# Two fused image layers on one core: the last image's output projection in strips of eight neighbouring rows, with the third image's fusion beside the last convolutions

## The chip, the cores and the metric

The kernel runs on one core of a Trainium2 chip. The metric is the device time of one execution in microseconds; "before" is the median of three runs. A profile is taken of one further execution. Engines: TensorE (PE: matrix products), VectorE (DVE), ScalarE (ACT), GpSimd (POOL) and SyncE (SP, which here only issues DMA transfers). Each engine works through its own instructions in order; POOL issues DMA transfers too.

## What is computed

All arrays are float32; x is (4, 512, 64, 64): four images. Layer 0 is a linear-attention block, layer 1 an edge-map block on its result. Cut to what matters:

```python
# layer 0 (64 heads of 8 channels)
qkv = 1x1 projections of x                                  # 1536 channels
pw  = grouped_1x1(depthwise_5x5(qkv))                       # the convolution branch, 64 more heads
f   = concat(qkv, pw) as (heads, 24, N)                     # 128 heads
query, key, value = relu(f[:8]), relu(f[8:16]), f[16:]
scores = [value; 1] @ key.T                                 # sums over all N = 4096 positions
out = (scores @ query)[:8] / (scores @ query)[8]            # per head and position
y   = batchnorm(proj_1x1(out, 1024 -> 512)) + x
# layer 1
sobel, lap, diag, grad = four 3x3 edge maps of each channel of y (square roots, absolutes, a maximum)
ef  = concat(gelu(bn(w_branch[k] @ map[k])) for the four maps)   # 4 x 128 channels
att = sigmoid(w_att2 @ gelu(w_att1 @ mean(ef over the image)))   # needs the whole image
z   = w_fuse @ (ef * att) + b_fuse
out = gelu(channel_layernorm(z)) + y
```

Two sums over a whole image order the work: `scores` must be complete before any position can be projected, and the mean of `ef` must be complete before the fusion `z` can begin.

## The kernel before

**Passes.** Sixteen passes, a `Group(b, g)` for each of four images and four groups of 16 heads. A pass runs over eight strips of 512 positions and does the 1x1 projections (`project`), the value products, the transposes (`turn`) and the scores. Its convolution branch runs one pass later: `rest()` lists 21 numbered steps (convolutions of KEY and QUERY by halves of the image, transposes `ctr`, correlations `corr`, denominators, `conv_divide`, folding with the projection weights) that are placed between the following pass's steps. After the last pass nothing follows, so the last group's 21 steps form a tail of their own (`tail`).

**Finished images.** For each image `stages()` makes three generators: `project_out` (the 1024 to 512 projection, with batch norm and residual; 8 strips of 4 output chunks), `edge_branches` (edge maps and the four branch products) and `fuse_out` (attention weights, fusion, layer norm, output). For the first three images they are advanced in small steps "behind" the next image's passes: each step of a pass costs a nominal time, `advance(t * pace)` adds it to an account, and background steps run while the account is positive. Their nominal shares are `SHARE_Y` 90, `SHARE_E` 450, `SHARE_F` 100 and some waits, 736 an image. One `pace` serves all passes from the second image on; it is set such that the third image's edges end within the tail and its fusion is left over.

**Last image.** After the tail the last image's stages run with `side="left"` in other tile pools, interleaved by hand: the first 16 of the 32 projection chunks alone, then the other 16 and the third image's fusion (`fill`, with the `FILL_` constants) between 16 edge steps, then the rest.

**Orders.** The order of instructions on PE is the order in which the program issues them. SP, POOL, DVE and ACT are ordered by a scheduler with priorities. `dve` and `act` are wrappers for operations put forward (all of them show as line 121), `nc.vector` and `nc.gpsimd` are plain.

**Strips.** x, and with it q, k, v, is held in strips of every fourth row: strip (half, k) is the rows k, k+4, ... of one half of the image, eight rows of 64. `project_out` goes by such strips: `load(j)` fetches `hd` (plain queries, from `flat_q`, one transfer of 1 MB) and four `chd` (convolved heads, from `cheads`, 256 KB each) and the residual `xr`; `attend(hd, 0)` is ReLU on ACT (L683), denominators `den` on PE (L686) and a reciprocal on DVE; `attend(hd, 1)` spreads the reciprocals by a product (`over`, L693) and multiplies `hd`. Then, for each chunk, eight products `yps` (L723), a scalar-tensor-tensor to `yt` and a store to `y` through POOL's queue (L734). `conv_divide` (around L576) is what writes `cheads`. The edges load windows `win` of neighbouring rows of `y` (L756), so with strips of every fourth row they need four strips of a half to be out first.

**Edges and fusion.** An edge step has eleven DVE instructions (L778 to L805), four on ACT (L792 to L806) and branch products `br` (L812, two groups of 3.43 us for one step of the last image); a GELU gives `ef_o`, stored to `ef` through POOL's queue (L825). The attention weights start with `hid_ps` (L897). The fusion has four product groups `zps` a strip (L929), a square `sq` on ACT, a copy `z`, running sums `total`, the product `var` (L945), a reciprocal `rstd` (L948), a scaling (L956), GELU (L957), the residual add with `yr` (L960) and the store (L961). For the third image (`b == B - 2`) the sums run on POOL and the copy `z` on ACT.

Of the kernel before, what the change touches and what calls it, by code (L numbers as in the profile page):

```python
# [70 lines left out]
FILL_Y, FILL_F = 6.9, 2.95  # L71
FILL_FIRST, FILL_ATT = 34.0, 18.0
FILL_EACH = (16 * FILL_Y + 40 * FILL_F - FILL_FIRST - FILL_ATT) / (4 * NJ // 2 - 1)

LEFT_E = 14.0
# [16 lines left out]
def conv_seq_kernel(  # L92
# [162 lines left out]
    class Group:  # L255
# [315 lines left out]
        def conv_divide(self, half):  # L571
            banks = self.spread_out(self.crec)
            for i in range(4):
                q = work_tile("cq")
                dve.tensor_mul(q, self.conv[QUERY][i], banks[i])
                nc.sync.dma_start(out=self.cheads[half, self.g, i], in_=q)  # L576
# [3 lines left out]
        def rest(self):  # L580

            h0, h1 = self.halves

# [12 lines left out]
            def roll(t, half):  # L596
# [10 lines left out]
                8: [cv(KEY, h1), roll(QUERY, h0)],  # L607
# [4 lines left out]
                13: [cv(QUERY, h0), roll(QUERY, h1)],  # L612
                14: co(h1, 1, 0),
                15: [*co(h1, 1, 2), own("conv_denominators", h0), own("mix")],
                16: [own("conv_weights")],
                17: [own("conv_divide", h0), own("conv_heads")],
                18: [cv(QUERY, h1), own("conv_fold")],
                19: [own("conv_denominators", h1)],
                21: [own("conv_divide", h1)],
# [28 lines left out]
    def project_out(b, ks, cheads, folded, side):  # L648
# [4 lines left out]
        with ExitStack() as stack:  # L653
            pool = stack.enter_context(tc.tile_pool(name=f"Y{b}", bufs=1, side=side, reuse_waits="tile"))
# [7 lines left out]
            def load(j):  # L662
                half, k = STRIPS[j]
                r, at = (k + 2) % 4, 8 * half + (k + 2) // 4
                q = pool.tile([P, NG, 512], F32, name="hd", tag="hd", bufs=3 if side == "right" else 2)
# [4 lines left out]
                for g in range(NG):  # L670
                    t = pool.tile([P, 512], F32, name="chd", tag="chd", bufs=6 if side == "right" else 4)
# [6 lines left out]
            def attend(hd, part):  # L678

                if part == 0:  # L680
# [6 lines left out]
                    recs[:] = [pool.tile([P, 512], F32, name="hrec", tag="hrec")]  # L687
# [3 lines left out]
                for g in range(NG):  # L691
                    q = slice(32 * g, 32 * g + 32)
                    nc.tensor.matmul(banks[g], lhsT=spread[q, :], rhs=recs[0][q, :], start=True, stop=True)  # L693
                for g in range(NG):
                    dve.tensor_mul(hd[g], hd[g], banks[g])

            recs = []
# [7 lines left out]
            ahead = load(1) if side == "right" else None  # L705
# [5 lines left out]
            for j, (half, k) in enumerate(STRIPS):  # L711
                hd = following
                following, ahead = ahead or (load(j + 1) if j + 1 < NJ else None), None
                if side == "right" and j + 2 < NJ:
                    ahead = load(j + 2)
                for c in range(NCH):
# [18 lines left out]
                    yield SHARE_Y / (NJ * NCH)  # L735

    def edge_branches(b, efs, pool_sb, side):

        y = ys[b % 2]
        with ExitStack() as stack:  # L740
# [24 lines left out]
            def edges(u, pair):  # L765
# [41 lines left out]
                if u + 1 < steps:  # L807
# [9 lines left out]
            def store(u, ks, parts):  # L817
# [7 lines left out]
                nc.gpsimd.dma_start(out=efs[wide * u // 512][:, ks[0] : ks[1] + 1 : step, at : at + wide], in_=o)  # L825
# [9 lines left out]
            if side == "left":  # L835

                load(0, 0)
                load(0, 1)
                banks = None
                for n in range(2 * steps + 1):  # L840
                    made = edges(n // 2, n % 2) if n < 2 * steps else None
# [31 lines left out]
    def fuse_out(b, efs, pool_sb, side):  # L873

        y = ys[b % 2]
        with ExitStack() as stack:
# [49 lines left out]
            def fuse(c, ef, zs, total, n):  # L926
# [6 lines left out]
                if b == B - 2:  # L933
# [4 lines left out]
                if c:  # L938
                    (dve if b == B - 1 else gps).tensor_add(total, total, sq)

            def norm(piece, zs, total):
# [8 lines left out]
                for c in range(NCH):  # L950
# [9 lines left out]
                    nc.gpsimd.tensor_add(rows(z), rows(z), rows(yr, WB)[:, :, 1 : W + 1])  # L960
# [5 lines left out]
            for piece in pieces + [None]:  # L966
                if piece:
# [9 lines left out]
                    fuse(0, ef, zs, total, n)  # L977
                    yield share
                    fuse(1, ef, zs, total, n)
# [3 lines left out]
                if piece and late:  # L983
                    fuse(2, ef, zs, total, n)
# [4 lines left out]
                if piece:  # L989
                    for c in range(3 if late else 2, NCH):  # L990
                        fuse(c, ef, zs, total, n)
# [3 lines left out]
    def stages(last, side="right"):  # L995
# [6 lines left out]
            project_out(b, ks, last.cheads, last.folded, side), edge_branches(b, efs, pool_sb, side),  # L1002
# [5 lines left out]
    for b in range(B):  # L1008
        cheads = dram.tile([2, NG, 4, P, 512], F32, name="cheads")
# [17 lines left out]
    def run(steps):  # L1027
# [9 lines left out]
    tail = [  # L1037
        (1, (4.0, 0.0)), (2, (2.0, 2.0, 2.0)), (3, (2.0, 2.0)), (4, (1.0, 1.0, 1.0)), (5, (1.0, 1.0)), (6, (1.0, 1.0)),
        (7, (1.0, 1.0)), (8, (4.0, 0.0)), (9, (2.0, 2.0, 2.0)), (10, (2.0, 2.0, 0.0)), (11, (1.0, 1.0)), (12, (1.0, 1.0)),
        (13, (4.0, 0.0)), (14, (1.0, 1.0)), (15, (1.0, 1.0, 2.0, 2.0)), (16, (3.0,)), (17, (3.0, 3.0)), (18, (6.0, 3.0)),  # L1040
        (19, (10.0,)), (21, (4.0,)),
    ]
    each = SHARE_Y + SHARE_E + SHARE_F + WAIT_Y + 2 * WAIT_E + WAIT_F + 6.0
    start = sum(t for t, _ in passes[NG]) - 3 * T_PROJ
    pace = ((B - 1) * each - SHARE_F - WAIT_F - 6.0 - LEFT_E) / (
        sum(t for steps in passes[NG:] for t, _ in steps) - start + sum(sum(v) for _, v in tail)
    )
# [10 lines left out]
    for n, steps in enumerate(passes):  # L1058
# [3 lines left out]
        run(steps)  # L1062
# [4 lines left out]
    for n, much in tail:  # L1067
        for (_, step), t in zip(others[n], much, strict=True):
            step()
            advance(t * pace)  # L1070
# [3 lines left out]
    projected, edged, fused = stages(last, "left")  # L1074
    next(edged)
    for _ in range(3):
        next(projected)
    while len(behind) > 1:
        if next(behind[0], None) is None:
            behind.pop(0)  # L1080
    next(behind[0])
    for n in range(NCH * NJ // 2):
        next(projected)
        if n in (4, 8, 12):
            next(behind[0])
    rest, spent, given = [projected] + behind, 0.0, 0.0

    def fill(much):

        nonlocal spent, given  # L1090
        given += much
        while rest and spent < given:
# [114 lines left out]
```

## Time and profile before

| | us |
|---|---|
| median of three runs (4747.78 to 4751.59) | 4748.3 |
| the profiled execution | 4767.75 |
| its span | 4765.8 |
| PE busy / DVE / ACT / POOL | 4523.5 / 2105.1 / 1619.2 / 1061.4 |
| mean granted TensorE clock | 0.975 |

The span runs from the first to the last instruction of the profiled execution. A profile's windows give each engine's busy time in a stretch, and the clock that TensorE was granted; its waits say which engine stood for whose result, and for how long in total; its groups give, for a line and an operation, the count, the busy time, the mean duration of one and the idle time just before them with what ended it. Where each stage begins is read off the timeline of PE: the first instruction of the last convolutions at 3887.46 us, the first `yps` of the last image at 4065.70, its last at 4346.2, the first `hid_ps` of the last image at 4598.97. PE's instructions come in records; a group of four 512-wide products is eight of them.

### The profile page before, as it was taken

What the parts mean: (1) busy time and instruction counts of PE and PEld (TensorE: products, weight loads), DVE (VectorE), ACT (ScalarE), POOL (GpSimd) and SP (SyncE); (2) the same over time, 40 slices, a digit from 0 to 9 for tenths busy, and PEclk for the clock granted to TensorE, in tenths of its full rate; (3) what the DMA queues carried; (4) which work ended last, traced back from release to release, by engine and by line L of the source; (5) the groups of instructions that cost most, each with busy time, mean ns of one, the idle gap of its engine ahead of it and who ended that gap; (6) DMA issues with size and microseconds to landing.
All of it is one profiled execution on the core that took longest, in us unless ns stands there. A gap on an engine that the chain in (4) does not pass through costs nothing. (4 is left out here: it accounts for less than half of the span.)

```text
span 4765.8 us, 85177 instructions
## 1 busy us (share of the span) xinstructions
PE 4523.5 (95%) x35900; PEld 2485.1 (52%) x35900; DVE 2105.1 (44%) x2788; ACT 1619.2 (34%) x2737; POOL 1061.4 (22%) x1387
## 2 busy tenths in 40 slices
PE   9999999999999999899999999999999996999787
PEld 5565554445666654444566665544455653443333
DVE  1212212225566535222466644323246565378666
ACT  1111111003554424200345553410034543136575
POOL 2121211111121125211111213511111121113543
PEclk9999999999999999999999999999999997999898
DMA  8677796656777776865687877786477776554345
GB/s 235 170 188 192 208 257 169 170 131 186 195 213 204 217 202 209 236 155 147 173 214 204 218 211 213 211 220 184 126 188 197 191 196 168 149 156 135 124 129 174
DMA packets 433388, 889.63 MB, mean 187 GB/s; under 512 B 181192, under 2 KB 213992, under 8 KB 414576
## 3 DMA queue, kind: packets, MB, share of 16 engines
q1 hardware_dynamic: 343024, 588.17, 45.9%
q0 software_dynamic: 89984, 296.03, 22.5%
q8 instruction: 283, 4.64, 0.4%
q14 instruction: 97, 0.79, 0.1%
HBM read 635.17 MB, written 248.84 MB: 185 GB/s over the span
## 5 line engine op out<-in xcount | busy, mean ns | idle before, releaser
L299 PE MATMUL proj<-xt,w_sb 128*128 128x512 f32 x2048 | 943.4, 604 | 8.8 <-DMA xt<-in_x 5.6
L299 PEld LDWEIGHTS proj<-xt,w_sb 128*128 128x128 f32 x2048 | 374.9, 191 | 451.1 <-issue 427.5
L418 PE MATMUL cv<-rolled,mat 64*32 64x504 f32 (+2 forms) x10240 | 559.0, 584 | 7.9 <-DMA rolled<-flatq 6.1
L327 PEld LDWEIGHTS val<-w_sb,xt 128*128 128x128 f32 x4096 | 480.5, 195 | 51.9 <-issue 35.7
L812 PE MATMUL br<-maps,wbr_sb 128*128 128x256 f32 (+1 forms) x1792 | 483.4, 424 | 22.6 <-ACT maps L806 10.2
L121 ACT COPY strip<-proj 128x512 f32<-128x512 f32 x256 | 149.5, 584 | 1037.0 <-PE proj L299 988.5
L929 PE MATMUL zps<-ef,wf_sb 128*128 128x512 f32 (+1 forms) x1056 | 461.7, 590 | 37.9 <-ACT z L121 22.8
L327 PE MATMUL val<-w_sb,xt 128*128 128x128 f32 x4096 | 494.2, 280 | 2.4 <-DVE kc_sb L121 1.8
L723 PE MATMUL yps<-chd,fold_sb 128*128 128x512 f32 x1024 | 465.9, 598 | 3.1 <-DVE s_sb L121 2.3
L723 PE MATMUL yps<-hd,fold_sb 128*128 128x512 f32 x1024 | 460.3, 592 | 0.0
L812 PEld LDWEIGHTS br<-maps,wbr_sb 128*128 128x128 f32 x1792 | 346.1, 196 | 168.1 <-issue 95.7
L121 DVE SCALAR_TENSOR_TENSOR yt<-yps,shift,xr 128x512 f32<-128x512 f32 x128 | 96.0, 751 | 725.3 <-PE yps L723 698.1
L418 PEld LDWEIGHTS cv<-rolled,mat 64*32 64x32 f32 x10240 | 197.7, 107 | 332.8 <-issue 326.5
L473 PE MATMUL corr<-near,ckt 128*32 128x160 f32 x8192 | 340.4, 315 | 15.4 <-ACT co L121 8.2
L929 PEld LDWEIGHTS zps<-ef,wf_sb 128*128 128x128 f32 x1056 | 200.8, 193 | 281.4 <-issue 226.9
L734 POOL DMA_DIRECT2D y<-yt x128 | 114.6, 895 | 960.0 <-DVE yt L121 839.1
L723 PEld LDWEIGHTS yps<-hd,fold_sb 128*128 128x128 f32 x1024 | 194.6, 190 | 244.9 <-issue 244.4
L723 PEld LDWEIGHTS yps<-chd,fold_sb 128*128 128x128 f32 x1024 | 188.9, 190 | 246.0 <-issue 227.6
L473 PEld LDWEIGHTS corr<-near,ckt 128*32 128x32 f32 x8192 | 265.4, 111 | 89.8 <-issue 54.1
L121 ACT ACTIVATE kt<-tr 128x512 f32<-128x512 f32 x128 | 75.9, 593 | 626.5 <-PE tr L351 468.8
L121 DVE COPY vt<-val 128x512 f32<-128x512 f32 x128 | 87.4, 683 | 392.0 <-PE val L327 382.4
L121 ACT ACTIVATE co<-cv 128x256 f32<-128x256 f32 (+1 forms) x384 | 162.3, 455 | 278.9 <-PE cv L418 256.1
(135 smaller groups left out, 5121.0 us busy)
## 6 DMA issues: line engine op xcount, KB each, us to landing
near<-near SPq DMA_DIRECT2D x256, 528.0 KB
xt<-in_x SPq DMA_DIRECT2D x172, 512.0 KB
rolled<-flatk POOLq DMA_DIRECT2D x256, 256.0 KB, 7.2
rolled<-flatq POOLq DMA_DIRECT2D x256, 256.0 KB, 7.4
win<-y SPq DMA_DIRECT2D x96, 396.0 KB
near<-vt SPq DMA_DIRECT2D x512, 66.0 KB
y<-yt POOLq DMA_DIRECT2D x128, 264.0 KB, 6.3
flatk<-strip POOLq DMA_DIRECT2D x128, 256.0 KB, 5.7
```

The source lines that it names most:

```text
L121: self.last = getattr(self.engine, name)(*args, **kwargs)
L299: nc.tensor.matmul(ps, lhsT=self.w[t][:, c, :], rhs=xs[self.b, j][c], start=(c == 0), stop=(c == NCH - 1))
L327: nc.tensor.matmul(ps[:, ts(c, P)], lhsT=xs[self.b, j][n][:, ts(c, P)], rhs=self.w[VALUE][:, n, :], start=(n == 0), stop=(n == NCH - 1),)
L418: nc.tensor.matmul(rows(banks[2 * s + i])[32 * j : 32 * j + 32, :, c0:c1], lhsT=self.mat[t][q, 4 * s + j, (dx + 2) * 4 : (dx + 2) * 4 + 4, :],
L473: nc.tensor.matmul(self.banks[jj][32 * i : 32 * i + 32, 160 * b : 160 * b + 160], lhsT=self.held["c", i][:, at : at + 32], rhs=v[:, 4 * n ...
L723: nc.tensor.matmul(ps, lhsT=fold_sb[g // NG][:, g % NG, ts(c, P)], rhs=hd[g], start=(n == 0), stop=(n == 2 * NG - 1),)
L734: nc.gpsimd.dma_start(out=y[c, :, at : at + 29 : 4, :], in_=yt)
L812: nc.tensor.matmul(rows(ps), lhsT=wbr_sb[:, k, c, :], rhs=rows(maps[:, slot[k], c % 2, :], WB)[:, :, 0:W], start=(c == 0), stop=(c == NCH ...
L929: nc.tensor.matmul(ps, lhsT=wf_sb[:, k, ts(c, P)], rhs=ef[k], start=(k == 0), stop=(k == 3))
```

## The change

- **Paces.** One pace for each image in place of one for all: 1.03 x 736 / 625.2 = 1.213 behind the second, third and fourth image's passes but the last, where 640 / 479.1 = 1.336 makes all but the third image's fusion proper end within the passes (before: 1.136).
- **Tail.** Beside the last group's 21 convolution steps stand 17 steps of the third image's fusion (`tail` now counts generator steps), and four more around the first `den` and `over` of the last projection: together 18 of its 32 `zps` groups and three norms. Before, the third image's last edges stood beside the convolutions.
- **Last projection.** A new `project_last` goes by strips of eight neighbouring rows. `hd`, `chd` and `xr` of a strip are put together from quarters of four old strips: four transfers each of 256 KB with runs of 512 bytes (before, `hd`: one of 1 MB with runs of 2 KB). `chd` is one tile of 1 MB with one buffer (before four of 256 KB). `y` is stored in two contiguous pieces of four rows a chunk (before one, rows four apart). The halves of the convolved queries are always taken in the order 0, 1.
- **`cheads` of the last image** has a new layout, and `conv_divide` writes it in 16 transfers of 32 partitions a half and group (before four); the last 16 on POOL's queue.
- **Order of the last image.** Edge steps begin after six chunks and then stand before every second chunk; ten of the 16 edge products lie among the chunks, six after the last one. Edge windows are loaded one step earlier, and the `ef` stores go through SP's queue. The rest of the third image's fusion (14 of its 32 `zps` groups) stands behind the projection.
- **Fusion of the third image.** The sums `total` run on DVE (before POOL). Of its first three strips the copies `z` run on DVE and the residual adds on POOL; of the other five the copies on ACT and the adds on DVE.

```diff
-                nc.sync.dma_start(out=self.cheads[half, self.g, i], in_=q)
+                if self.b < B - 1:
+                    nc.sync.dma_start(out=self.cheads[half, self.g, i], in_=q)
+                    continue
+                for j in range(4):
+                    at = 32 * i + 8 * j
+                    (nc.gpsimd if self.g == NG - 1 and half else nc.sync).dma_start(
+                        out=self.cheads[half, :, self.g, at : at + 8, :], in_=q[32 * j : 32 * j + 32, :]
+                    )
...
+    def project_last(b, ks, cheads, folded):
...
+            def plain(s):
+                q = pool.tile([P, NG, 512], F32, name="hd", tag="hd", bufs=2)
+                for k in range(4):
+                    r, at = (k + 2) % 4, 2 * s + (k + 2) // 4
+                    nc.sync.dma_start(
+                        out=q[:, :, ts(k, P)], in_=flat_q[b % 2][:, r, :, at : at + 2, :].rearrange("g p b w -> p g (b w)")
+                    )
+                return [q[:, g, :] for g in range(NG)]
+
+            def convolved(s):
+                q = pool.tile([P, NG, 512], F32, name="chd", tag="chd")
+                for k in range(4):
+                    nc.sync.dma_start(
+                        out=q[:, :, ts(k, P)], in_=cheads[s // 4, 3 - k, :, :, ts(s % 4, P)].rearrange("g p x -> p g x")
+                    )
+                return [q[:, g, :] for g in range(NG)]
...
+            for s in range(NJ):
+                hd, following = following, plain(s + 1) if s + 1 < NJ else None
+                for c in range(NCH):
+                    xr = pool.tile([P, 512], F32, name="xr", tag="xr", bufs=4)
...
+                    for n in range(2 * NG):
+                        g = (n + (NG if c else 0)) % (2 * NG)
+                        nc.tensor.matmul(
+                            ps, lhsT=fold_sb[g // NG][:, g % NG, ts(c, P)], rhs=(hd + chd)[g],
+                            start=(n == 0), stop=(n == 2 * NG - 1),
+                        )
+                    if following and c in (0, 2):
+                        attend(following, c // 2)
...
+                    for n in range(2):
+                        at = 8 * s + 4 * n + 1
+                        nc.gpsimd.dma_start(
+                            out=y[c, :, at : at + 4, :], in_=yt.rearrange("p (k n) w -> p n k w", k=4)[:, n]
+                        )
+                    if following and c == NCH - 1:
+                        chd = convolved(s + 1)
+                    yield 0.0
...
-                nc.gpsimd.dma_start(out=efs[wide * u // 512][:, ks[0] : ks[1] + 1 : step, at : at + wide], in_=o)
+                (nc.sync if side == "left" else nc.gpsimd).dma_start(out=efs[wide * u // 512][:, ks[0] : ks[1] + 1 : step, at : at + wide], in_=o)
...
-                if b == B - 2:
+                if b == B - 2 and j >= LATE_Z:
                     act.activation(z, ps, AF.Identity, bias=fbias[:, c : c + 1])
...
-                    (dve if b == B - 1 else gps).tensor_add(total, total, sq)
+                    (dve if late else gps).tensor_add(total, total, sq)
...
-                    nc.gpsimd.tensor_add(rows(z), rows(z), rows(yr, WB)[:, :, 1 : W + 1])
+                    (nc.vector if b == B - 2 and j >= LATE_Z else nc.gpsimd).tensor_add(
+                        rows(z), rows(z), rows(yr, WB)[:, :, 1 : W + 1]
+                    )
...
+    tail = {
+        1: (2, 0), 2: (0, 1, 0), 3: (1, 0), 4: (0, 0, 0), 5: (0, 0), 6: (0, 0), 7: (0, 0), 8: (2, 0),
+        9: (0, 1, 1), 10: (0, 0, 0), 11: (0, 0), 12: (0, 0), 13: (2, 0), 14: (0, 0), 15: (0, 0, 2, 0), 16: (0,),
+        17: (0, 0), 18: (2, 0), 19: (2,), 21: (1,),
+    }
+    whole = sum(t for steps in passes[NG : 2 * NG] for t, _ in steps)
+    paces = [1.03 * each / whole] * (B - 1) + [(each - LEFT_F) / (whole - start)]
...
+    next(edged)
+    for count in (1, 1, 2):
+        next(projected)
+        fill(count)
+    for n in range(NJ * NCH // 2):
+        if n == 3 or n >= 4:
+            next(edged)
+        next(projected)
+        next(projected)
+    next(projected, None)
+    next(fused)
+    for _ in range(5):
+        next(edged)
+        fill(2)
+    next(edged)
     for _ in range(3):
         next(fused)
-        fill(FILL_ATT / 3)
-    for stage in rest + [fused, edged]:
+        fill(2)
+    for stage in (third, fused, edged):
         for _ in stage:
             pass
```

`fill(count)` advances the third image's fusion by that many steps.

## The prediction

> **What bounds the kernel now.** First the page: PE is busy 95% of the span and the other engines less than half, so the end is set by TensorE's work, its pauses and its clock.
>
> ```profile
> PE 4523.5 (95%) x35900; PEld 2485.1 (52%) x35900; DVE 2105.1 (44%) x2788; ACT 1619.2 (34%) x2737; POOL 1061.4 (22%) x1387
> PE   9999999999999999899999999999999996999787
> PEclk9999999999999999999999999999999997999898
> ```
>
> The forty slices show PE solid until the last six. Idle in the span is 4765.8 − 4523.5 = 242 us; by the PE timeline some 140 of it lie after 3880 us. So I read that part by windows (columns: PE, PEld, DVE, ACT, POOL busy with counts; granted clock; DMA share; GB/s):
>
> ```profile
> 3880.00:3920.00 40.00, 33.38 (x407) 22.49 (x410) 18.56 (x31) 18.98 (x41) 6.76 (x12) 0.91 0.60 150
> 3960.00:4000.00 40.00, 29.22 (x424) 16.39 (x430) 24.89 (x37) 10.15 (x16) 4.93 (x9) 0.83 0.51 128
> 4000.00:4040.00 40.00, 25.86 (x194) 11.72 (x178) 23.69 (x32) 23.86 (x35) 2.46 (x7) 0.75 0.53 175
> 4280.00:4320.00 40.00, 40.00 (x102) 16.71 (x101) 37.46 (x32) 22.01 (x20) 3.98 (x5) 1.00 0.43 129
> 4360.00:4400.00 40.00, 31.00 (x73) 13.42 (x71) 36.66 (x31) 24.63 (x29) 28.13 (x3) 0.95 0.47 157
> 4440.00:4480.00 40.00, 17.50 (x41) 7.46 (x40) 29.69 (x24) 23.20 (x27) 24.43 (x11) 0.80 0.29 91
> 4720.00:4766.00 46.00, 12.77 (x44) 8.85 (x44) 23.20 (x31) 22.67 (x32) 16.13 (x16) 0.72 0.45 131
> ```
>
> By the first instruction of each stage on the PE timeline this is four stages: A, last convolutions, 3887.5 to 4065.7 (178.2 us, 50.9 idle, clock down to 0.75); B, last projection, to 4359.9 (294.2, PE full at clock 1.00); C, third image's fusion and nine edge products, to the last image's attention weights (`hid_ps`) at 4599.0 (239.0); D, last fusion, to 4765.8 (166.8). What ends PE's pauses there is in the waits after 3880 us (total, times, longest); the last line is from 1900 to 2000 us:
>
> ```profile
> PE zps L929 <- ACT z L121: 22.8, 2, 20.3
> PE ctr L445 <- ACT co L121: 13.4, 2, 7.2
> PE var L945 <- POOL total L121: 10.7, 2, 9.5
> PE br L812 <- ACT maps L806: 10.2, 2, 8.0
> PE den L686 <- ACT hd L683: 6.9, 1, 6.9
> ...
> PE den L686 <- ACT hd L683: 14.0, 1, 14.0
> ```
>
> In A short chains (copy, mask, divide) leave PE nothing to do; in C it waits for elementwise work of the fusion and of the edge maps. The durations I use are in the groups of 3990 to 4766 us:
>
> ```profile
> L929 PE MATMUL zps<-ef,wf_sb 128*128 128x512 f32 x480 | 216.3, 607 | 29.9 <-ACT z L121 22.8 <-ACT rstd L121 4.9 <-DVE wf_sb L121 1.3
> L121 POOL TENSOR_TENSOR total<-total,sq 128x512 f32<-128x512 f32 x24 | 89.0, 3707 | 62.4 <-ACT sq L121 62.0
> L948 DVE RECIPROCAL rstd<-rstd 128x512 f32<-128x512 f32 x15 | 50.3, 3351 | 29.2 <-ACT rstd L121 29.2
> L785 DVE TENSOR_TENSOR maps<-dv 128x2110 f32<-128x2110 f32 x16 | 38.6, 2415 | 0.0
> L803 DVE TENSOR_TENSOR maps<-maps 128x1052 f32<-128x1052 f32 x16 | 20.0, 1249 | 44.8 <-ACT maps L802 44.8
> ```
>
> **The change, part by part.** The unit on PE is a group of four 512-wide products (eight records), 3.43 us on the timeline at full clock.
>
> (1) *Passes, up to the last convolutions.* The steeper pace brings ten edge-product groups of the third image ahead of 3887.5: +10 × 3.43 = +34.3. It also leaves a rest between an image's fusion and the next image's `project_out`: the waits of `den` on `hd` at 1958 (14.0) and 3127 (4.1) should fall to the 2 us of the first image, which has no fusion just ahead: −14. From 3480 to 3888 PE idles 27 us under background work whose density rises 7% (from 1.136 to 1.213) in the first passes and 18% (to 1.336) in the last; DVE and POOL sit at half or below, and this costs little by itself, but four times as many `cheads` stores stand in SP's queue: between 0 and 27 (idle doubled), I take 13. Start of the convolutions: 3887.5 + 34 − 14 + 13 = 3921 (bounds 3903 to 3949).
>
> (2) *A'.* PE work: convolution groups 4 × 8.6, correlations 20.3, 18 `zps` groups 61.7, transposes, folds and three norm products 17: 133. Fusion now fills the holes that A had. What stays: small gaps 7, slow clock 8, and one large gap ahead of the first `den`. Its price: the `hd` load stands on SP behind `yr` loads, these wait for buffers that POOL's residual adds (1.25 each) free, and those stand behind 16 `cheads` stores on POOL's queue (0.53 to 0.90 us an issue by `rolled` and `y`: 8 to 14 us). The old 1 MB `hd` load took 9.8 us from issue (4024.4) to relu (4034.2). I take 20 in all, so A' = 133 + 7 + 8 + 20 = 168 (bounds 150 with the load wholly ahead, 190 with both delays added). The totals' adds move from POOL to DVE here and in (4), 24 × 1.05 = 25 us; DVE has 19 to 25 busy of 40 in A and takes them.
>
> The Trainium skill, "TensorE: Matmul & The Clock Gate", Part 1, says an idle window of about 3.4 us halves the clock until as long a busy stretch has passed. This trace agrees in kind: `den` took 4.66 us for eight records after 6.9 us of pause, where 1.07 is normal. By the rule the large gap would cost some 3.4 / 2 = 1.7 us more, an estimate from that page.
>
> (3) *B'.* 32 chunks × 6.87 = 219.8; seven attends × 3.1 (1.07 + 2.03) = 21.7; ten edge products × 6.87 = 68.7: 310. Before, seven products lay here and nine behind. The new `chd` has one buffer. At strips 1 and 2 its load has only 6.87 us of `hd` products as cover, later 13.7, since an edge product lies between. A 256 KB transfer with 2 KB runs (`out<-z`) lands in 3.7 us, one with 264-byte runs (`y<-yt`) in 6.1 to 6.3, `rolled` 7.2; four issues on SP take 2.85. So 512-byte runs land in 6.5 to 10 us after release: 0 to 3 at the early two, plus `den` catching up with its load; I take 12 for all (bounds 0 and 35). B' = 322. DVE per strip: two edges × 15.4 (eleven instructions), four `yt` × 0.75, divide 4.04, four `hd` × 0.68 = 40.6, with 2.2 an edge waiting on L802 45.0, against PE's 44.3 with two products: level, as at 4280 to 4320 (37.5 of 40 with PE full).
>
> The skill's page "DMA: Bandwidth & Descriptors", Bandwidth and Specifications, speaks against this step: batch to 1 MiB or more, with runs of at least 512 bytes. The new loads are at that edge, a quarter as large. Its fixed 2.0 us a transfer, paid four times in a row for `hd`, would be 6 us more a strip, an estimate; nothing here shows whether they overlap.
>
> The other edits of this stage: 64 `y` stores instead of 32 on POOL, +32 × 0.89 = 28 us, hidden by POOL's 3.5 to 4 busy of 40 there (uncovered, 2 × 0.89 a chunk would still fit in 6.87); four `xr` loads a strip on SP and the edge loads one edge ahead, with a whole edge of 15 us as cover; the `ef` stores moved to SP, where each waits for a GELU with `hd`, `chd` and `xr` loads queued behind it: a late GELU makes those late, which is part of the 35 above.
>
> (4) *C', last `yps` to `hid_ps`.* Before 252.8 (4346.2 to 4599.0). Now PE has 14 `zps` groups less eight and six products, 71; DVE sets it: four edges 61.6, mean 2.3, five totals × 1.05, two reciprocals 6.7, seven scalings × 0.8, five residual adds (0.9 by its other tensor-tensor rows), 86; ACT waits 8; then the last root 3, product 6.9, GELU and pooling 6: 110 (bounds 90 with DVE ahead, 130 with it an edge behind). The slow POOL totals (3.71, 89 us in all) are gone.
>
> (5) *D'.* 166.8, plus four more third-image groups behind `hid_ps` (six instead of two), 13.7 and a norm 1: 182 (bounds 170 if they hide in the chain through the attention, 195).
>
> Sum: 3921 + 168 + 322 + 110 + 182 = 4703, 63 under the span of 4765.8. The profiled execution took 4767.75, the runs' median is 4748.3, 0.4% lower; I put the difference on the median: **4685**. PE's work is the same; 63 is under half of the 140 idle us.
>
> **Rivals.** *Loads starve the strips* (the other side). If four loads of 512-byte runs go one after another at `rolled`'s 7.2 us, `chd` needs 29 and the cover is 7 to 14: 15 to 22 at each boundary. For: one buffer, and SP carries `xr`, `win`, `ef` too. Against: DMA moved 333 GB/s in the first 40 us, while B' asks for some 6 MB in 44 us. At 13 for each of seven boundaries, 91 less the 12 in the sum, +79: 4764. It decides from (4757.8 − 4685) / 7 = 10 us a boundary.
> *DVE becomes the bound of B'.* 45.0 is already over 44.3; one further ACT wait of 2 us an edge over 12 edges gives +25: 4710. For: the 44.8 us on L803. Against: PE stayed full at 94% DVE.
> *It doesn't do what it says*: fusion beside the convolutions isn't hidden, because POOL's stores, SP's `yr` and `hd` stand in line. A' becomes 200 to 220: 4717 to 4737. For: that chain of queues; against: the other image transitions cost 4 to 14.
> *Better*: no gap at `den` (−20), and 5 less at the strips: 4660.
>
> **How the numbers follow.** Forecast (4668 to 4700) 0.42, better 0.12, DVE 0.17, not hidden 0.15, starved 0.10, mishaps I don't see 0.04. A change under 0.2% (9.5 us) can't be told from none: same, 4738.8 to 4757.8, takes the top of "not hidden" and the bottom of "starved", 0.07; slower the rest of those and the unseen, 0.13; faster 0.80. The range: the bounds of (1) to (5) as independent errors give −37 and +49 (root of the sum of squares); downward I take that, 4648; upward 4745, which takes in "not hidden" too.
>
> **What would show it.** Right: last convolutions begin near 3921; A' has one gap, at `den`; PE near 40 of 40 in B' with DVE near 37; last `yps` to `hid_ps` near 110; no long `den` wait at images 1 and 2. Wrong: waits of `yps` on `chd` loads above 10 us each, A' over 190, or DVE waits inside B'.

## The result, and the profile after

The changed kernel takes 4773.2 us (median of 4 runs, 4769.4 to 4776.4) against 4748.05 for the kernel before: a ratio of 1.0048, 95% interval [1.0036, 1.0061]. It is slower by half a per cent; 4685 was forecast. Its profiled execution took 4774.8 us with a span of 4773.1, 7.3 longer than the span of before. (That execution of before was 19.45 above its own median, this one 1.6 above its own, so the two spans show only 7.3 of the 25 us by which the medians differ; stages compared with before, below, carry that difference.)

Start with the page of the changed kernel, the lines of busy time and of the forty slices:

```profile
PE 4523.5 (95%) x35900; PEld 2482.6 (52%) x35900; DVE 2132.5 (45%) x2844; ACT 1629.6 (34%) x2735; POOL 972.2 (20%) x1375
PE   9999999999999899999999989989999899799987
PEclk9999999999999999999999999999999999899999
```

PE is as busy as before to a tenth of a microsecond, with the weak slices in other places: the ones at the end are fewer, and more eights stand in the middle. The stages, read off the timeline of PE as for the prediction (the last row from the first `hid_ps` of the last image to the end of the span):

| | before | predicted | after |
|---|---|---|---|
| last convolutions begin at | 3887.4 | 3921 | 4004.5 |
| A, to the first `yps` of the last projection | 178.3 | 168 | 171.9 |
| B, to the end of its last `yps` | 280.7 | 322 | 323.9 |
| C, to `hid_ps` | 252.6 | 110 | 91.2 |
| D, to the end | 166.8 | 182 | 181.7 |
| A to D | 878.4 | 782 | 768.6 |

The end of the program came out as predicted, 13 us better even. All of the miss, and more, lies ahead of it: the last convolutions begin 83 us later than predicted, 117 later than before, and only 34 of that is product work brought forward. Up to that point PE is idle for 162.3 us where it was 99.2 before. What it waited for, in the waits of the whole span (total, times, longest):

```profile
PE hid_ps L1004 <- DMA watt_sb<-in_watt: 37.9, 3, 17.0
PE den L786 <- ACT hd L783: 28.0, 3, 24.6
PE cden L564 <- ACT co L120: 16.9, 4, 7.3
PE over L701 <- DVE hrec L120: 12.5, 3, 4.2
PE val L326 <- DMA w_sb<-in_wqkv: 11.5, 1, 11.5
PE corr L472 <- ACT co L120: 11.0, 2, 5.5
PE den L693 <- ACT hd L690: 6.7, 3, 2.2
```

The same products in the kernel before, up to its last convolutions (0 to 3887.4 us):

```profile
PE den L686 <- ACT hd L683: 20.3, 3, 14.0
PE over L693 <- DVE hrec L121: 1.1, 2, 0.6
PE hid_ps L897 <- DMA watt_sb<-in_watt: 0.5, 1, 0.5
```

`hid_ps` opens an image's fusion; its three waits are those of the first three images, in the ninth, thirteenth and sixteenth pass, and in the kernel before it waited 0.5 us for these weights in all. `over` follows `den` in an image's first attend; three times the same 4.2. These two are at the handover from one background stage to the next. The waits of `cden` and `corr` are in the pass's own convolution branch. `den L693` on the contrary did what was predicted: 6.7 where it was 20.3. The long `den L786` (24.6) is the gap ahead of the last projection, in A.

The idle time pass by pass says the same. Of the passes from the sixth to the sixteenth, those in which a stage of an image begins or ends (6, 9, 10, 13, 14, 16) hold 53 us of idle PE before and 121 after; those with edges alone (7, 8, 11, 12, 15) hold 33 and 31, though the background in them is denser: by 7% in the first four, by 18% in the fifteenth (in the code 1.336 stands behind all four passes of the fourth image). In these passes the steeper pace as such costs nothing.

How a handover looks, on the timeline of the changed kernel (start, duration, engine, line, instruction, idle before it and what ended it):

```profile
1654.94 1.15 SPq L457 DMA_DIRECT2D near<-near  x2
1656.14 1.05 SPq L289 DMA_DIRECT2D xt<-in_x  x2
1657.24 0.60 SPq L986 DMA_DIRECT2D wf_sb<-in_wfuse  x1
1657.88 0.47 SPq L988 DMA_DIRECT2D watt_sb<-in_watt  x1
1672.22 0.99 PE L1004 MATMUL hid_ps<-pooled,watt_sb 128*64 128x1 f32 x8 [17.02 <-DMA watt_sb<-in_watt]
1673.13 6.69 PE L298 MATMUL proj<-xt,w_sb 128*128 128x512 f32 x8
...
3129.26 3.47 PE L693 MATMUL den<-hd,ks_sb 128*32 128x512 f32 x8 [2.23 <-ACT hd L690]
3136.91 2.09 PE L701 MATMUL over<-hrec,consts_sb 32*128 32x512 f32 x8 [4.17 <-DVE hrec L120]
```

PE was at `hid_ps` at 1655.2 us, before SP had even issued the load that it needs: the load stands on SP behind `near` loads (what the correlations read), which left only when a correlation product had just ended on PE (1654.9), and behind 1 MB of `xt` and 1 MB of `wf_sb`. And the pause has a price beyond its length: the eight `proj` records after it took 6.69 us (3.60 undisturbed), `den` 3.47 (1.07). Between `den` and `over` there is no work of the pass at all: the copy and the reciprocal in between need 4.0 us of DVE (0.69 + 3.35), and PE stands.

In A to D the windows bear out the prediction (columns: PE, PEld, DVE, ACT, POOL busy with counts; granted clock; DMA share; GB/s):

```profile
4140.00:4180.00 40.00, 20.61 (x49) 7.99 (x50) 14.66 (x13) 13.27 (x21) 13.12 (x22) 0.70 0.89 278
4360.00:4400.00 40.00, 40.00 (x102) 16.73 (x102) 33.26 (x29) 19.12 (x21) 5.97 (x8) 1.00 0.51 126
4540.00:4580.00 40.00, 32.71 (x71) 13.99 (x71) 39.26 (x34) 33.40 (x34) 0.00 (x0) 0.91 0.19 64
4720.00:4773.00 53.00, 19.84 (x77) 13.64 (x75) 30.02 (x39) 25.38 (x36) 17.90 (x18) 0.79 0.49 146
```

The first holds the gap at `den`; in the second PE is full beside two edge products a strip; in the third DVE is nearly full (39.3 of 40), as (4) had it; the last is the chain of outputs that also ended the kernel before.

### The profile page after: what moved, and what is told of

It reads as the page before. It is cut to its first block, busy times and chain, and to the rows that moved or that the text cites. A ratio compares the mean times of both kernels' runs of the same rounds, so it can differ in the third digit from the quotient of the medians.

```text
span 4773.1 us, 85417 instructions
## 1 busy us (share of the span) xinstructions
PE 4523.5 (95%) x35900; PEld 2482.6 (52%) x35900; DVE 2132.5 (45%) x2844; ACT 1629.6 (34%) x2735; POOL 972.2 (20%) x1375
## 5 line engine op out<-in xcount | busy, mean ns | idle before, releaser
L917 PE MATMUL br<-maps,wbr_sb 128*128 128x256 f32 (+1 forms) x1792 | 473.3, 417 | 16.2 <-ACT maps L911 11.2
L1036 PE MATMUL zps<-ef,wf_sb 128*128 128x512 f32 (+1 forms) x1056 | 459.5, 586 | 10.5 <-DVE z L120 5.6
L732 PE MATMUL yps<-chd,fold_sb 128*128 128x512 f32 x768 | 352.3, 602 | 4.5 <-DVE yt L120 3.7
L732 PE MATMUL yps<-hd,fold_sb 128*128 128x512 f32 x768 | 345.2, 592 | 0.0
L732 PEld LDWEIGHTS yps<-hd,fold_sb 128*128 128x128 f32 x768 | 146.1, 190 | 183.5 <-issue 183.3
L743 POOL DMA_DIRECT2D y<-yt x96 | 85.7, 892 | 758.9 <-DVE yt L120 651.8
L732 PEld LDWEIGHTS yps<-chd,fold_sb 128*128 128x128 f32 x768 | 143.1, 192 | 183.5 <-issue 168.1
```

The lines of the kernel that those rows point to most:

```text
L732: nc.tensor.matmul(ps, lhsT=fold_sb[g // NG][:, g % NG, ts(c, P)], rhs=hd[g], start=(n == 0), stop=(n == 2 * NG - 1),)
L743: nc.gpsimd.dma_start(out=y[c, :, at : at + 29 : 4, :], in_=yt)
L917: nc.tensor.matmul(rows(ps), lhsT=wbr_sb[:, k, c, :], rhs=rows(maps[:, slot[k], c % 2, :], WB)[:, :, 0:W], start=(c == 0), stop=(c == NCH ...
L1036: nc.tensor.matmul(ps, lhsT=wf_sb[:, k, ts(c, P)], rhs=ef[k], start=(k == 0), stop=(k == 3))
```

## The experiments

Two theories to begin with. *Handovers*: the new paces put the stage boundaries at unlucky places of a pass, where a product comes before the load or the reciprocal that it needs. *Density*: more background a pass costs in itself. Ratios are to the kernel before, with their 95% intervals; a change of under 5 us between two experiments isn't read as one. "Start" is the time at which the last convolutions begin; it and "A to D" are of the one profiled execution, which lies up to 10 us off its run's median (e2 9.7 above, e13 9.9 below).

| run | median us | ratio | start | A to D |
|---|---|---|---|---|
| changed kernel | 4773.2 | 1.0048 [1.0036, 1.0061] | 4004.5 | 768.6 |
| e1, fusion later behind its loads | 4748.7 | 0.9995 [0.9985, 1.0005] | 3985.9 | 765.1 |
| e2, old pace for two images | 4732.7 | 0.9962 [0.9948, 0.9976] | 3945.4 | 795.3 |
| e3, one pace | 4817.4 | 1.0140 [1.0122, 1.0159] | 4024.2 | 796.6 |
| e4, attend spaced | 4744.8 | 0.9991 [0.9979, 1.0004] | 3975.6 | 762.0 |
| e5, e4 + weights on POOL's queue | 4718.3 | 0.9933 [0.9912, 0.9954] | 3951.4 | 766.8 |
| e6, e4 + adds on DVE | 4741.0 | 0.9980 [0.9969, 0.9991] | 3972.5 | 760.2 |
| e7, e2 + e4 | 4722.0 | 0.9936 [0.9913, 0.9960] | 3934.7 | 789.7 |
| e8, e5 + `yr` on POOL's queue | 4715.1 | 0.9931 [0.9918, 0.9944] | 3952.8 | 762.8 |
| e9, e7 + weights on POOL's queue | 4709.8 | 0.9918 [0.9904, 0.9932] | 3919.0 | 792.7 |
| e10, e5 + norm behind `den` | 4710.9 | 0.9919 [0.9902, 0.9937] | 3957.5 | 758.4 |
| e11, e9 + norm behind `den` + adds on DVE | 4718.1 | 0.9932 [0.9913, 0.9951] | 3915.9 | 797.7 |
| e12, kernel before + both early edits | 4769.5 | 1.0043 [1.0030, 1.0055] | 3881.2 | 881.0 |
| e13, e9 + norm behind `den` | 4722.2 | 0.9949 [0.9936, 0.9963] | 3915.3 | 795.2 |

**e1.**

```diff
-            yield 14.0
+            yield 28.0
             if b == 0:
...
-    paces = [1.03 * each / whole] * (B - 1) + [(each - LEFT_F) / (whole - start)]
+    paces = [1.03 * each / whole] * (B - 1) + [(each + 14.0 - LEFT_F) / (whole - start)]
```

> The changed kernel with the first product of the attention (hid_ps) 14 units of background later behind the loads of its weights (28 instead of 14), the pace of the last image raised by the same 14 units so that the order from the last convolutions on stays. Theory 'transitions' (the changed passes lose time where one stage hands over to the next, because PE reaches a product before the loads queued on SP have landed): the three waits of hid_ps on the watt_sb loads (17.0 + 12.5 + 8.4 = 37.9 us in the changed kernel) fall below 5 together, and with the slow clock behind each the time falls 35 to 45 us, to about 4732. Theory 'density' (a steeper pace as such costs): nothing is gained, 4773 within 5, the idle time turns up elsewhere.

The kernel gained 24.5 us, but not where handovers had it: `hid_ps` still waited 14.3 and 14.8 us for the first and the second image (1689 and 2866 us); only the last wait was gone. The loads had moved along with the product: SP issued them at 1676.6, 32 us after the sum over the edges (1644.6), again right behind `near` loads. More background between load and product doesn't help when SP's order puts the load late. What was gained beside it shows in other passes (idle in the fourteenth 10.7 after 21.2), where later stages fell in other places. Half a miss.

**e2.**

```diff
-    paces = [1.03 * each / whole] * (B - 1) + [(each - LEFT_F) / (whole - start)]
+    paces = [1.136] * (B - 1) + [0.0]
+    paces[-1] = ((B - 1) * each - LEFT_F - 1.136 * (2 * whole - start)) / whole
```

> The changed kernel with the old pace of 1.136 behind the second and third image's passes and 1.372 behind the last one's, so that the same work is done when the last convolutions begin. Theory 'transitions': the second and third image's passes run as in the kernel before (the third image's passes end near 2740 us, where the changed kernel is 45 us later), and the fourth image's lose at its own transitions only: 4773 - 30 to - 60, about 4730. Theory 'density': the 1.372 costs in the last image what 1.213 and 1.336 cost in all three, and the time stays within 10 us of 4773.

4732.7, 40.5 less than the changed kernel, as handovers had it. The thirteenth pass begins at 2747 us, 4 later than in the kernel before (2743; 2791 in the changed kernel). With 1.372 behind the last image its third and fourth pass idle 6.1 and 4.5 us (12.2 and 21.8 in the changed kernel with 1.336): density is out. But A to D grew by 27: a new wait of 21.5 us stands in A, the last convolution's for its `rolled` loads (the rolled queries that it reads).

**e3.**

```diff
-    paces = [1.03 * each / whole] * (B - 1) + [(each - LEFT_F) / (whole - start)]
+    paces = [((B - 1) * each - LEFT_F) / (3 * whole - start)] * B
```

> The changed kernel with one pace of 1.221 for all three images: the same work at the same mean density, but with no rest between images, so that the stages of the three images meet the passes in three different places. Theory 'transitions', in the form that the fixed place in the pass is what is unlucky (the same gaps of 2.23, 4.17, 5.5 and 7.3 us recur for each image): some of the gaps go, 4745 to 4765. Theory 'density': within 5 of 4773.

44 us slower, which neither theory expected. The same mean density, with other gaps: `ksum_ps` waits 25.7 us for `ktotal` (3 times), `cden` 33.1, `hid_ps` 24.7; two of the third image's edge products are left over and stand ahead of the last convolutions, and in C an edge product of the last image waits 25.3 us for its maps near 4589. Two of the three waits of `ksum_ps` (9.3 and 7.1) lie in passes with edges alone, whose idle time is 51 us here and 31 in the changed kernel, though behind the second and third image the pace hardly differs (1.221 and 1.213). So it isn't only the handovers: where background work falls between the pass's own steps decides too, in both directions and by tens of microseconds.

**e4.**

```diff
-            yield 0.7 * WAIT_Y
+            yield 0.5 * WAIT_Y
             attend(following, 0)
-            yield 0.2 * WAIT_Y
+            yield 0.4 * WAIT_Y
             attend(following, 1)
```

> The changed kernel with the denominators of each image's first strip 6.4 units earlier and so 6.4 more between them and the spreading product (0.5 and 0.4 of the wait instead of 0.7 and 0.2). Theory 'transitions': the three waits of over on hrec (4.17 each) go, 10 to 18 us with the slow clock behind them, about 4759, unless den now waits longer for its hd load (then no gain, and den's wait grows from 2.2 to about 8).

28.5 us gained, more than the waits themselves (ten runs in two clumps, 4739 to 4742 and 4747 to 4759; the profiled one is of the first), and most of it ahead of the last convolutions (start 3975.6 after 4004.5). The second image's attend shows how; the pass's transposes and a convolution now stand between the two products, and `over` doesn't wait:

```profile
1921.51 3.47 PE L693 MATMUL den<-hd,ks_sb 128*32 128x512 f32 x8 [7.84 <-ACT hd L690]
1924.92 1.12 PE L350 MATMUL tr<-consts_sb,strip 128*128 128x128 f32 x4
1925.96 8.95 PE L417 MATMUL cv<-rolled,mat 64*32 64x512 f32 x160
1934.85 1.14 PE L701 MATMUL over<-hrec,consts_sb 32*128 32x512 f32 x8
```

`den` waits longer, as the expectation's other branch had it, but only here. Why the two stood back to back: a step of a pass is credited with its nominal time at once, and a convolution's 9.2 × 1.213 = 11.2 units pay a wait of 6.4 in one go; 12.8 they don't. Of the 28.9 us by which the start came earlier, 18.3 are idle time (162.3 to 144.0) and 10.6 shorter records: PE was busy 3830.2 us up to there with the same instructions, 3840.8 in the changed kernel.

**e5.** On top of e4:

```diff
-            nc.sync.dma_start(out=wf_sb, in_=wfuse)
             watt1_sb = pool.tile([P, NCH, 64], F32, name="watt1_sb", tag="sq", bufs=3)
-            nc.sync.dma_start(out=watt1_sb, in_=watt1)
+            nc.gpsimd.dma_start(out=watt1_sb, in_=watt1)
             watt2_sb = pool.tile([64, C], F32, name="watt2_sb", tag="sq", bufs=3)
-            nc.sync.dma_start(out=watt2_sb, in_=watt2)
+            nc.gpsimd.dma_start(out=watt2_sb, in_=watt2)
+            nc.gpsimd.dma_start(out=wf_sb, in_=wfuse)
```

> The kernel of e4 with the three loads of the fusion's weights issued from POOL's queue instead of SP's, the small ones first. Theory 'SP's order' (hid_ps waits because the loads stand on SP behind the near loads, which wait for correlations that PE runs just ahead of hid_ps): the three waits of hid_ps (13.6, 12.3, 8.9 in e4) fall to a few us, the time by 25 to 40 us to about 4712. Theory 'the transfer itself is slow' (14 us from issue to landing, the 1 MB load ahead of the small ones): only a part goes, 5 to 15 us.

26.4 us less than e4, start 3951.4 after 3975.6: about what "SP's order" had for the time. In the timeline of e5 the load leaves just ahead of the product instead of after it, and ahead of the big one:

```profile
1644.86 0.54 POOL L987 DMA_DIRECT2D watt_sb<-in_watt  x1
1651.74 0.98 PE L1004 MATMUL hid_ps<-pooled,watt_sb 128*64 128x1 f32 x8 [5.26 <-DMA watt_sb<-in_watt]
```

Two of the three waits are left, 14.7 together (34.7 in e4, three), not the few us that were expected. At this handover the wait fell from 17.0 in the changed kernel to 5.3: 4.3 because the load left 1.6 us before PE stood at the product and not 2.7 after, 7.5 because it landed in 6.9 us and not in 14.3 behind `wf_sb`. So the landing, which the other theory named, is the larger part; queue and sequence were changed together, and which of the two did it isn't told apart.

**e6.** On top of e4: `LATE_Z = 2` for 3.

> The kernel of e4 with the third image's strip 2 handled as the strips behind it (its residual adds on DVE, its copies z on ACT), so that no yr load on SP waits for an add that stands on POOL behind the 16 stores of cheads. Theory 'SP behind POOL' (the prediction's chain for the gap ahead of the last projection): the wait of den on hd (23.9 us) falls by 8 to 12 us and the time with it, to about 4734. Theory 'the load sets it': the gap stays at 22 to 25 us and the time within 3 of e4.

4741.0 for 4744.8, the wait of `den` 21.7 for 23.9: the prediction's chain for this gap (SP behind POOL's adds behind POOL's stores) isn't what sets it. SP still sat 20.8 us at six `yr` loads, until 4110.6; only then came `hd`. SP's own waits say why: in e4 these loads wait 22.3 us for POOL's adds (longest 10.5), in e6 10.8 for DVE's (longest 10.6) and 9.6 for POOL's. The longest wait went from one engine to the other at the same length, since both adds wait for the same norm; the adds of strip 1, still on POOL, e6 left as they were.

**e7.** e2 and e4 together.

> The kernel of e2 (old pace for two images, 1.372 behind the last) with the spacing of e4. If the losses of the stage boundaries are independent of each other and of the pace, the gain of e4 comes in full at the three boundaries: e2 - 20 to - 30, about 4708. If the gain of e4 came from where its pieces happened to fall in the pass, it doesn't add: 4725 to 4740.

4722.0: 10.7 less than e2, half of what independent losses would give. Where `den` was late already (17.6 in e2, 15.3 here) a wider distance behind it gains little.

**e8.** On top of e5:

```diff
-                    nc.sync.dma_start(
+                    (nc.gpsimd if b == B - 2 else nc.sync).dma_start(
                         out=yr, in_=y[c].rearrange("p r w -> p (r w)")[:, at * WB : (at + high) * WB]
```

> The kernel of e5 with the third image's yr loads (residual of the fusion) issued from POOL's queue instead of SP's. e6 left the 24 us gap ahead of the last projection as it was, so either SP is held by the yr loads whatever engine adds (they wait for the norm chain: root, reciprocal, scaling, GELU, add), or the hd load itself takes that long. Theory 'SP held by yr': with them off SP the hd load is issued some 20 us earlier, right behind the store of the folded weights, the wait of den on hd falls from 24 to below 8 and the time by 14 to 20 us, to about 4701. Theory 'the load itself': the gap stays above 18, 4715 to 4722.

`hd` was issued 23.5 us earlier (4070.8 for 4094.3), and nothing was gained. The timeline of e8 says why:

```profile
4070.76 2.10 SPq L764 DMA_DIRECT2D hd<-flatq  x4
4092.41 0.69 ACT L120 ACTIVATE z<-zps,fbias 128x512 f32<-128x512 f32 x1 [5.58 <-DMA out<-z]
4094.41 0.69 ACT L120 ACTIVATE rstd<-var,ln_eps 128x512 f32<-128x512 f32 x1
4099.25 2.93 ACT L1064 ACTIVATE z<-z,vec_sb 128x512 f32<-128x512 f32 x4 [2.85 <-DVE z L1063]
4102.08 2.17 ACT L783 ACTIVATE hd<-hd 128x512 f32<-128x512 f32 x4
4102.75 3.47 PE L786 MATMUL den<-hd,ks_sb 128*32 128x512 f32 x8 [21.84 <-ACT hd L783]
```

The load leaves at 4070.8, but its ReLU stands on ACT behind the third image's norm: copies `z` that wait for buffers (`out` stores), the root, the scaling on DVE, four GELUs. The wait moved from SP to ACT, at nearly the same length (21.8 for 24.3). Both theories fall, though the numbers of the second came out; the norm of strip 2 holds both queues.

**e9.** e7 with the weights' loads of e5.

> The kernel of e7 (old pace for two images, 1.372 behind the last, spacing of e4) with the weights' loads on POOL as in e5. If losses at the boundaries add, the two remaining waits of hid_ps (12.8 and 6.6) fall below 5 together and the time from 4722 to about 4708. If the pace decides only where pieces fall, the gain at hid_ps is given back elsewhere: 4717 to 4727.

4709.8, as expected for losses that add (`hid_ps` waits 4.9 in all), and the start is 3919.0, near the 3921 that the prediction had. A to D still carries the 20 us in front of the last convolution (20.3 for `rolled`; these loads stand on POOL behind residual adds that wait for GELUs and `yr` loads).

**e10.** On top of e5:

```diff
-    for count in (1, 1, 2):
+    for count in (0, 2, 2):
```

> The kernel of e5 with the step that holds the third image's norm of strip 2 moved behind the last image's first den (steps 0, 2, 2 in place of 1, 1, 2). e8 took the yr loads off SP and the hd load came 36 us before den, yet the ReLU of hd then stood on ACT behind that norm's GELUs, so the gap stayed at 22 us. Theory 'the norm chain' (root, reciprocal, scaling, GELU, add stand ahead of hd's load on SP and of its ReLU on ACT): with the norm behind den both are free, den waits for the load alone, below 10 us, and the time falls 12 to 18 us, to about 4703. Theory 'it moves': the same wait turns up at the reciprocal or at the first yps, within 5 us of e5's 4718.

```profile
4088.97 2.88 SPq L764 DMA_DIRECT2D hd<-flatq  x4
4097.16 2.19 ACT L783 ACTIVATE hd<-hd 128x512 f32<-128x512 f32 x4 [6.38 <-DMA hd<-flatq]
4097.84 3.47 PE L786 MATMUL den<-hd,ks_sb 128*32 128x512 f32 x8 [12.42 <-ACT hd L783]
```

In e10 the ReLU waits for its load alone and the gap is halved, 12.4 for 24.3; A shrinks from 168.9 to 159.3, and the median by 7.5. The rest is the `yr` loads of the norm before, on SP ahead of `hd`.

**e11.** e9 with e10's order and `LATE_Z = 0`.

> The kernel of e9 with the order of e10 and with all residual adds of the third image on DVE and all its copies z on ACT, so that no rolled load on POOL stands behind an add that waits for a GELU (20.3 us of the last convolution's wait in e9). If both gaps close: 4710 - 12 - 15, about 4683. If DVE, which then carries all sums and adds, or ACT becomes late in their place: 4695 to 4710.

A miss: 4718.1. `rolled` (20.7) and `den` (21.0) wait as in e9; the adds on DVE left the stores of `out` and the norm as late as they were, and the wait for an `ef` load at 3937 is 8.3 (5.1 in e9).

**e12.** The kernel before with the edits of e4 and e5.

> A control: the kernel before (old pace, old end) with the spacing of e4 and the weights' loads on POOL as in e5. Theory 'the steeper paces made the boundaries late' (in the kernel before PE waited 0.5 us for these weights and 1 us for hrec): these two edits find little to gain here, 4740 to 4750, and what e9 gains over the kernel before comes from the new end of the program. Theory 'the edits are good by themselves': 4700 to 4725, and the new end is worth little.

20 us slower than the kernel before, which neither theory expected. In the profiles, start 3881 and A to D 881 are near those of before (3887 and 878), whose execution was 19 above its own median, so where the 20 us lie can't be read. By themselves the two edits gain nothing; in the changed kernel they recover what the new paces had lost, and what e5, e9 and e10 gain over the kernel before lies in the new end of the program (e9: start 32 us later than before, A to D 86 shorter).

**e13.** e9 with e10's order alone.

> The kernel of e9 with the norm of strip 2 behind the first den, as in e10, and nothing else (e11 had two edits at once and closed neither gap). If e10's gain of some 8 us is the order of the norm, it comes here too: den's wait from 20.6 to about 12, 4700 to 4705. If e11's failure was this order's: den still waits about 21, 4708 to 4715.

No gain, but a loss of 12 us (4722.2; five runs between 4712 and 4730, the profiled one the fastest); `den` still waits 21.4. Here `hd` is issued at 4080.5, and PE stands at `den` from 4068 on: the last convolution was late by 19.4 for `rolled`, and less of the fusion seems to be left ahead of `den`. So e10's gain needs e10's paces, and e11 didn't fail by its adds alone. The 20 us at `rolled` in e2, e7, e9, e11 and e13 were not closed by any run; that POOL's adds cause them is read from the timeline, not shown by an edit.

## Why the prediction was wrong

- **What bounds the kernel**: right as far as it went. PE's work stayed the same, and its pauses set the time. But only those after 3880 us were looked at closely; the 99 us before it were taken as given.
- **(1), passes**: the step that failed. Predicted: +34 of work, −14 at `den`, +13 for density and the `cheads` stores, 3921 with bounds 3903 to 3949. Measured 4004.5. The work and the −14 came true (`den` 20.3 to 6.7). Where the sum has 13, the runs have some 97: 77 of other idle time and 20 of longer records. The 13 was priced from the wrong things. Density costs nothing (33 and 31 us idle in the edge-only passes before and after), and neither do the stores as far as the runs show: e9 keeps them and idles 23 us in the fourteenth to sixteenth pass, before 27. (The 27 us that the working gives for 3480 to 3888 are 19 in the windows, 408.0 less 388.8.) What the working left out is that a pace also sets the distance between two steps of one stage, and so whether `hid_ps` finds its load (+37 us; e5 takes 20 of 35 away) and `over` its reciprocal (+11; e4 takes all away); `w_sb`, `cden` and `corr` add 29 by the waits, and no run takes these up one by one. So idle time rose by 63 instead of falling by one; the other 20 are records at a lower clock behind the pauses, and 2 us of the third image's attention products. With the old pace, spaced attends and the weights off SP (e9) the step lands at 3919, but not by the predicted terms: `den` waits 21.9 there, so the −14 is missing.
- **(2), A'**: 171.9 for 168. The size was right, the gap 24.6 for 20, its cause only partly: the `yr` loads do stand ahead of `hd` on SP, but they wait for adds that wait for the norm, whichever engine adds (e6), and the norm's chain on ACT holds the ReLU as well (e8, e10).
- **(3), B'**: 323.9 for 322, of which PE is busy 318.9 and idle 5, where the sum had 310 and 12; that the total fits is partly luck. The strips' loads cost 2.4 + 1.0 us at `den` at the early boundaries. The objection of the Trainium skill ("DMA: Bandwidth & Descriptors", Bandwidth) does show in the load itself, though not in the time. In two pairs in which ACT waited for the load alone, the 1 MB load of before and then the four of after:

```profile
4094.56 0.38 SPq L666 DMA_DIRECT2D hd<-flatq  x1
4100.95 2.19 ACT L683 ACTIVATE hd<-hd 128x512 f32<-128x512 f32 x4 [31.76 <-DMA hd<-flatq]
...
4369.90 2.01 SPq L764 DMA_DIRECT2D hd<-flatq  x4
4378.30 2.19 ACT L783 ACTIVATE hd<-hd 128x512 f32<-128x512 f32 x4 [8.13 <-DMA hd<-flatq]
```

From the first issue to the ReLU these are 6.4 and 8.4 us; in all such pairs of the two runs' last projections 5.9 to 6.7 and 7.2 to 9.1. So four loads with 512-byte runs take some 2 us longer, not the 6 of the estimate, and the work ahead of `den` hides nearly all of it. The 9.8 us that the prediction took for the old load are no landing time: ACT was busy with edge work until 4034.2 and began the ReLU then.
- **(4), C'**: 91.2 for 110, at the bound "with DVE ahead" (90). DVE is nearly full in one window (39.3 of 40); over the stage it is busy 77.9 and PE 79.5, and PE's only waits are 11.2 for edge maps, so DVE sets less than the sum had. (Its 71 of PE work come out with 14 groups less six, not less eight.)
- **(5), D'**: 181.7 for 182.
- **Rivals**: none of them was it. Starved strips, DVE in B' and a fusion not hidden are each contradicted by the stage's own time; the chance that went to "mishaps I don't see" was 0.04. The rival that should have stood there is one mechanism: a new pace moves every handover, of three images, to another place of the pass; its price could have been bounded from the row `den` <- `hd` (14.0 for one) times six handovers, 84.
- **The sum onto the median**: the span of before was 19 us above its median's execution, that of after was not. Even a right sum of spans would have missed by some 18 us; of the 88 by which 4685 was off, 70 are the sum's.

## What to carry over

When background work is laid beside a main loop by an account, a new pace isn't only a density: list, for each handover, the product, the load or reciprocal that it needs, and what stands between them on PE and ahead of them on the queue, and price every one; the pass's own short chains belong on the list too (`ksum_ps` and `cden` in e3). Here a wait for a load that stood late on its queue was cut by another queue and sequence (e5) and not by more work ahead of the product (e1); a wait for a short chain on DVE was cured by distance (e4). Where two queues led to the same instruction (SP's load, ACT's ReLU), freeing one of them gained nothing (e8). The end of a change can be right while its beginning pays for it: e9 and e10 keep the new end and are faster than both kernels, at 0.992 of the time before.

## What was not expected of the hardware

A long pause of PE cost some 3.4 us beyond its length. After the 24.6 us gap `den` took 3.47 us instead of 1.07 and the next `zps` group 4.47 instead of 3.60, 3.3 more together; after the 17.0 us one `hid_ps` took 0.99 instead of 0.63 and the `proj` group 6.69 instead of 3.60, 3.5 more. After only 2.2 us `den` took 3.47 too: the granted clock is 1.00 up to that pause and 0.56 from 760.6 to 764.1, and 0.50 again at the `over` that follows 4.2 us of pause (768.3 to 770.3). The estimate from the Trainium skill ("TensorE: Matmul & The Clock Gate", Part 1) was 1.7 us for the large gap, from an idle window of about 3.4 us; here 2.2 us of pause behind a convolution were enough. So small pauses cost more than their sum, which is part of why e4 gained 28.5 us where the waits that it was aimed at summed to 12.5.
